# The root and reciprocal of a grouped RMS norm on four rows of 128 tokens, spread by way of DRAM, and a gate's Silu issued with the next eviction

## The chip, the cores and the metric

The kernel runs on one core of a Trainium2 chip. The metric is device time in microseconds (us), the median of repeated executions. Five engines run their own instruction streams: TensorE (PE in the profile, its weight loads PEld), VectorE (DVE), ScalarE (ACT), GpSimd (POOL) and SyncE (SP). In this kernel SP issues every DMA, in the order in which the program gives them to it.

## The reference

The input x is 2048 tokens by 1024 features. After a layernorm, two branches are added to it: a Mamba-2 block (64 heads of 64, 8 groups, state size 128, convolution over 4 tokens) and a base layer with a routed low-rank part. Cut to what matters here:

```python
proj = xn @ in_proj_w.T                     # gate 4096 | conv input 6144 | dt 64
xBC  = silu(causal_conv4(hbc) + conv_bias)
dt   = softplus(dt + dt_bias);  dA = exp(-exp(A_log) * dt)
state_t = state_{t-1} * dA_t + dt_t * x_t (outer) B_t
y_t  = state_t . C_t + D * x_t
# per group of 512 features and per token:
yn = y / sqrt(mean(y**2) + 1e-5) * norm_weight
yn = yn * silu(gate)
out = x + yn @ out_proj_w.T + (xn @ W_base.T + b_base + lora(xn))
```

The change touches the line of `yn = y / sqrt(...)` and the place where `silu(gate)` is computed.

## The kernel before

Features lie on partitions, tokens along the free axis. The sequence is cut into 2 parts s of 1024 tokens, each into 2 halves of 512 (TB) and 8 chunks of 128 (Q). A *block* is one (s, group, half): 32 blocks in order, each with four *slots* c = 0 to 3, one for each chunk of 128 tokens.

**The projection.** The in_proj matrix product runs as a stream of "products" of a seven-product scheme (Winograd's form of Strassen's). One product is four matmuls of 128x512 in f32, which the profile shows as 8 passes and some 3.4 to 3.6 us. The seven write three PSUM tiles (`ps_a`, `ps_x`, `ps_y`, with a suffix for what is computed: `x` conv input, `g` gate, `b` base; pool `ps_proj`, four buffers) in the order a1, x6, y5, a2, x7, y3, x4. A finished quarter of the result is *evicted* by `stored(...)`: for one quarter ACT applies the function straight to PSUM (L529); for the other three DVE adds a kept sum (L531) and, for the gate, ACT applies Silu in place (L533); then SP stores the tile (pool `ev`, four buffers) to DRAM. The last product of a tile triple, x4, needs the PSUM bank after the eviction behind x7.

**A slot.** Each slot holds four or five products. The loop over slots writes, in order: product 1 with its side work; in slot 0 the mean of the norm of the *previous* block (`norm_mean`); `scan_b`, the scan's matmuls of this chunk: 16 passes `ps_y`, 8 passes `ps_e`, and the state update `ps_st`; the loads of later decays (`load_decays`: `dab`, 512 KB spread to all partitions, and `ecp`, 2 x 128 KB); then the steps of `scan_a` for the next chunk (scan `es` on DVE L688; `ps_cb` and its copies on ACT L698, L700; `dab` on DVE L702; transposes `ps_xt`, the eight copies `xdt` scaled by dt on ACT L713, `xdd` on POOL L83) between products 2, 3 and 4. dt itself comes out of a softplus that DVE and ACT compute for a coming piece of the sequence (a polynomial from L318 on) spread over slots of the first half.

**Order.** PE's instructions keep the order of the program (`mm`, `transpose`). So do ACT's xdt copies and the conv's Silus, and in the second half of the sequence (s = 1) the POOL operations of `gp`. The remaining instructions of DVE, ACT and SP are put in order by a planner; the order is then fixed for each engine. The pool `ps_one` has one buffer for each of the tags "aux", "y", "e" and "st"; an instruction that writes into a tile of such a tag waits until all readers of the previous tile of that tag are done.

**The norm.** In the last slot of a block, `norm_squares` adds D x to y (into the tile xg of the conv) and sums the squares of the four 128-feature rows. In slot 0 of the next block `norm_mean` sums over partitions with one matmul against a 128x128 matrix of ones (f32, two passes, `ps_nv` in tag "aux"), which leaves the same 512 sums on all 128 partitions; ACT takes the root (L809). `norm_gate`, a generator advanced step by step with the side work of later products, takes the reciprocal (DVE L815), multiplies the four rows of xg (L818) and then multiplies by the gate (`sg`, L826), two rows at a time, each pair stored to DRAM as y. xg has two buffers (pool `p2`): the conv two blocks on first writes its buffer again with ACT (L640), DVE finishes it (L646). 

After about 2710 us of the profiled execution the second phase begins: out_proj, in a two-level form of the same scheme, with the low-rank part. The change doesn't touch it.

The functions that the change touches, and what calls them:

Of the kernel before, what the change touches and what calls it, by code (L numbers as in the profile page):

```python
# [8 lines left out]
F32 = mybir.dt.float32  # L9
AF = mybir.ActivationFunctionType  # L10
# [17 lines left out]
P = 128  # L28
TS = 1024
NS = L // TS  # L30
TB = 512
Q = 128
NQ = TB // Q
# [9 lines left out]
def mamba_lora_kernel(  # L43
# [17 lines left out]
    nc = tc.nc  # L61

    dram = ctx.enter_context(tc.tile_pool(name="dram", bufs=1, space=bass.MemoryType.DRAM))
    const = ctx.enter_context(tc.tile_pool(name="const", bufs=1))
# [6 lines left out]
    ps_one = ctx.enter_context(tc.tile_pool(name="ps_one", bufs=1, space=bass.MemoryType.PSUM))  # L71
    scan_ctx = ExitStack()
    p1 = scan_ctx.enter_context(tc.tile_pool(name="p1", bufs=1))
# [4 lines left out]
    def mm(*args, **kw):  # L78
        tc.keep_in_program_order(nc.tensor.matmul(*args, **kw))  # L79
# [11 lines left out]
    ones = const.tile([P, P], F32, name="ones")  # L91
    nc.vector.memset(ones, 1.0)
    ident = const.tile([P, P], F32, name="ident")
    make_identity(nc, ident)
    eps = const.tile([P, 1], F32, name="eps")
    nc.vector.memset(eps, EPS)


# [42 lines left out]
    nw = p1.tile([P, INNER // P], F32, name="nw")  # L141
# [151 lines left out]
    def small_mm(ps, x_of):  # L293
        for k in range(KT):
            mm(ps, x_of(k), wsm[:, k, :], start=(k == 0), stop=(k == KT - 1))
# [201 lines left out]
    def plain_pair(key, name, quarters, quarter):  # L497
# [22 lines left out]
            quarter(m, n, ps, rstd_of[n], ALU.mult)  # L520
        yield

    def stored(to, first_tile, s, func):


        def quarter(m, n, ps, add, alu=ALU.add):
            e = ev.tile([P, TB], F32, tag="ev", name="ev")
            if add is None:
                nc.scalar.activation(e, ps, func)  # L529
            else:  # L530
                nc.vector.tensor_tensor(e, ps, add, alu)  # L531
                if func != AF.Copy:
                    nc.scalar.activation(e, e, func)  # L533
            at = s * TS + n * TB
            nc.sync.dma_start(to[:, first_tile + m, at : at + TB], e)

        return quarter

# [66 lines left out]
    def steps(gen, n):  # L605

        return [lambda: next(gen, None) for _ in range(n)]


    xbc_of = {}  # L610
# [170 lines left out]
    def load_gate(s, g, half):  # L781
        sg = p1.tile([P, 4, TB], F32, tag="sg", name=f"sg_{s}_{g}_{half}")
        at = s * TS + half * TB
        nc.sync.dma_start(sg, gate_d[g][:, :, at : at + TB])
        sg_of[s, g, half] = sg

    norm_of = {}
# [14 lines left out]
        yield  # L802

    def norm_mean(s, g, half):
        y = y_of[s, g, half]
        ps = ps_one.tile([P, TB], F32, tag="aux", name=f"ps_nv_{s}_{g}_{half}")
        mm(ps, ones, y[:, 0, :], start=True, stop=True)
        std = p1.tile([P, TB], F32, tag="rms", name=f"rms_{s}_{g}_{half}")
        nc.scalar.activation(std, ps, AF.Sqrt, bias=eps, scale=1.0 / (4 * P))  # L809
        norm_of[s, g, half] = std  # L810

    def norm_gate(s, g, half):

        xg, std = xbc_of[s, g, half][0], norm_of[s, g, half]
        nc.vector.reciprocal(std, std)  # L815
        yield
        for j in range(4):
            nc.vector.scalar_tensor_tensor(  # L818
                xg[:, j, :], xg[:, j, :], nw[:, 4 * g + j : 4 * g + j + 1], std,
                ALU.mult, ALU.mult,  # L820
            )
        yield
        at = s * TS + half * TB
        for j in (0, 2):
            two = xg[:, j : j + 2, :]
            nc.vector.tensor_tensor(two, two, sg_of[s, g, half][:, j : j + 2, :], ALU.mult)  # L826
            nc.sync.dma_start(y_d[g][:, j : j + 2, at : at + TB], two)
            yield
# [137 lines left out]
    def target(slot):  # L966
        for (s0, p0), (s1, p1_) in zip(plan, plan[1:]):
            if slot <= s1:
                return p0 + (p1_ - p0) * (slot - s0) // (s1 - s0)
# [4 lines left out]
    for b, blk in enumerate(blocks):  # L974
        s, g, half = blk
        prev = blocks[b - 1] if b else None
        nxt = blocks[b + 1] if b + 1 < len(blocks) else None

        i, stage = divmod(b - 2, 3)
        piece, after = (1, i), stage  # L980
        if not (s == 0 and 0 <= i < NQ):
            piece = after = None
        if b == 14:
            ln_ctx.close()
            wo_ctx = ExitStack()
            wo = wo_ctx.enter_context(tc.tile_pool(name="wo", bufs=1, reuse_waits="tile"))
        if b == 15:
            base_left = left_sums
        if 0 <= b - 15 < 16:
            left_sums = out_sums(wo, b - 15)  # L990
        for c in range(NQ):
            slot += 1
            n = target(slot) - done
            follow = (*blk, c + 1) if c + 1 < NQ else (*nxt, 0) if nxt else None
            second = (*blk, c + 2) if c + 2 < NQ else (*nxt, c + 2 - NQ) if nxt else None
            side = []
            if c == 0 and nxt:
                side += [lambda: load_raw(*nxt)]
            if after == 0 and c == 1:
                load_piece(*piece, "sg", p1)  # L1000
                ln = ln_next(*piece)
            if after == 0 and c == 2:
                side += steps(ln, 3)
            if after == 0 and c == 3:
                side += steps(ln, 4)
            if after == 1 and c in (0, 2, 3):
                side += steps(rest, 1)
            if c in (1, 2) and nxt:
                if c == 1:
                    conv_steps = conv(*nxt)  # L1010
                side += steps(conv_steps, 4)
            if c == 2 and after != 0:
                side += [lambda: load_gate(*blk)]
            if b == 1 and c < 2:

                js = range(4) if c == 0 else range(4, 7)
                side[:0] = [
                    lambda j=j: nc.sync.dma_start(xop_d[0][j], ops_of["x", 0][j]) for j in js
                ]
            a = scan_a(*follow) if follow else iter(())  # L1020
            parts = [side[i * len(side) // n : (i + 1) * len(side) // n] for i in range(n)]

            products(1, parts[0])
            if c == 0 and prev:
                norm_mean(*prev)
            scan_b(*blk, c)
            if b == 14 and c:
                next(left_sums)
            if 0 <= b - 15 < 16 and c:
                next(left_sums)  # L1030
            if second:
                load_decays(*second)
            next(a, None)
            if c == 0 and prev:
                out = norm_gate(*prev)
                parts[1:4] = [[*p, lambda: next(out, None)] for p in parts[1:4]]
                parts[3] += [lambda: next(out, None)] * 2
            if c == NQ - 1:
                sq = norm_squares(*blk)
                parts[1] += steps(sq, 2)  # L1040
                parts[2] += steps(sq, 1)
            products(1, parts[1])
            next(a, None)
            products(1, parts[2])
            products(1, parts[3])
            next(a, None)
            if after == 0 and c == 1:
                next(ln)
            for i in range(4, n):
                products(1, parts[i])  # L1050
            if b == 14:
                left_sums = base_sums(wo, c)
                next(left_sums)
            if 0 <= b - 15 < 16 and c == 0:
                if b == 15:
                    next(base_left)
                next(left_sums)
            if after == 0 and c == 2:
                next(ln)
            if after == 0 and c == 3:  # L1060
                sm = lp.tile([P, 2, NSM], F32, tag="sm", name=f"sm_{piece[0]}_{piece[1]}")
                ps = ps_one.tile([P, 2, NSM], F32, tag="st", name=f"ps_sm_{piece[1]}")
                for h in range(2):
                    small_mm(ps[:, h, :], lambda k: piece_of[piece][:, k, h, :])
                nc.scalar.copy(sm, ps)
                rest = small(*piece, slice(piece[1], 2 * NQ, NQ), sm, home)
                load_gate(*blk)
            if (after, c) in ((1, 1), (2, 0)):
                next(rest)
    norm_mean(*blocks[-1])  # L1070
    for _ in norm_gate(*blocks[-1]):
        pass
# [157 lines left out]
    for t, (s, p) in enumerate(passes):  # L1230
        last = t + 1 == len(passes)
        for u, i in enumerate(units):
# [89 lines left out]
            for n, j in enumerate(inner):  # L1322
                w = w_ready.pop(0)
                ps = {1: pa, 2: pa, 6: px, 7: px, 4: px, 5: py, 3: py}[j]
                for q in range(2):
                    for k in range(KH):
                        mm(
                            ps[:, q, :], w[:, q, k, :], ops[j][:, k, :],
                            start=(n < 3 and q + k == 0), stop=(k == KH - 1), skip_group_check=True,
# [69 lines left out]
```

## Time and profile before

| | us |
|---|---|
| median of 3 runs | 3456.07 (3455.59 to 3456.18) |
| profiled execution | 3459.94 |
| its span, first to last instruction | 3458.2 |
| mean granted PE clock | 0.996 of full speed |
| PE busy | 3409.4, 12818 instructions |
| DVE busy | 2530.2 |
| ACT busy | 926.4 |
| POOL busy | 832.3 |
| DMA | 769.79 MB, mean 223 GB/s |

The profile is one execution with the time of each instruction. Rows of groups give the line, engine, operation, output and inputs by the program's names, shapes, count, busy time, mean duration in ns, and behind the last bar the idle time before them with what ended it. Rows of waits give who waited for whom: us in total, times, longest. The chain is followed back from the last instruction to whatever released each step. "issue" is time in which the engine waited for nothing that the profile shows. In a DMA row the last figure is the median time from issue to landing.

### The profile page before, as it was taken

What the parts mean: (1) busy time and instruction counts of PE and PEld (TensorE: products, weight loads), DVE (VectorE), ACT (ScalarE), POOL (GpSimd) and SP (SyncE); (2) the same over time, 40 slices, a digit from 0 to 9 for tenths busy, and PEclk for the clock granted to TensorE, in tenths of its full rate; (3) what the DMA queues carried; (4) which work ended last, traced back from release to release, by engine and by line L of the source; (5) the groups of instructions that cost most, each with busy time, mean ns of one, the idle gap of its engine ahead of it and who ended that gap; (6) DMA issues with size and microseconds to landing.
All of it is one profiled execution on the core that took longest, in us unless ns stands there. A gap on an engine that the chain in (4) does not pass through costs nothing.

```text
span 3458.2 us, 37638 instructions
## 1 busy us (share of the span) xinstructions
PE 3409.4 (99%) x12818; PEld 1993.4 (58%) x12818; DVE 2530.2 (73%) x2861; ACT 926.4 (27%) x2158; POOL 832.3 (24%) x571
## 2 busy tenths in 40 slices
PE   9999999999999999999999999999999999999999
PEld 7444544544545554444555555444445588888888
DVE  7548787877887877677888887777885466566665
ACT  2223343333433333323333333333331000000000
POOL 3133323233333211332332433322332000000000
PEclk9999999999999999999999999999999999999999
DMA  6546655655656676787787788787777687585644
GB/s 234 189 164 201 209 178 189 206 191 197 199 193 205 197 262 220 246 283 231 240 251 245 234 260 253 234 255 226 244 233 270 236 279 242 198 299 188 213 165 145
DMA packets 530319, 769.79 MB, mean 223 GB/s; under 512 B 35152, under 2 KB 264656, under 8 KB 527440
## 3 DMA queue, kind: packets, MB, share of 16 engines
q1 hardware_dynamic: 530128, 767.39, 68.6%
q8 instruction: 102, 1.67, 0.2%
q14 instruction: 89, 0.73, 0.1%
HBM read 516.64 MB, written 250.61 MB: 222 GB/s over the span
## 4 chain that ended last, share of the span: by engine, by line
PE 77%; DVE 10%; issue 6%; DMA 4%; POOL 2%; ACT 1%; SPq 0%; POOLq 0%; DVEq 0%; ACTq 0%
PE ps_x_x L79 10%; PE ps_x_w L79 8%; PE ps_a_x L79 7%; PE ps_y_x L79 7%; PE ps_x_g L79 6%; PE ps_a_w L79 6%; PE ps_y_w L79 6%; PE ps_y_g L79 4%; PE ps_a_g L79 4%; PE ps_y L79 3%; PE ps_e L79 3%; PE ps_x_b L79 2%; PE ps_st L79 2%; PE ps_a_b L79 2%; PE ps_y_b L79 2%
## 5 line engine op out<-in xcount | busy, mean ns | idle before, releaser
L688 DVE TENSOR_TENSOR_SCAN es<-dab,here 128x1024 f32<-128x1024 f32 x128 | 327.3, 2557 | 285.8 <-POOL xdd L83 264.6
L83 POOL TENSOR_TENSOR xdd<-xdt,es 128x512 f32<-128x512 f32 x128 | 145.3, 1135 | 1003.4 <-ACT xdt L713 967.6
L646 DVE SCALAR_TENSOR_TENSOR xg<-rawx,cw,xg 128x512 f32<-128x512 f32 x384 | 339.8, 934 | 22.3 <-ACT xg L640 21.7
L79 PE MATMUL ps_x_w<-t,w 128*128 128x256 f32 x1344 | 303.8, 379 | 0.0
L79 PEld LDWEIGHTS ps_x_w<-t,w 128*128 128x128 f32 x1344 | 255.4, 190 | 41.5 <-issue 7.7
L713 ACT ACTIVATE xdt<-ps_xt,dt 128x64 f32<-128x64 f32 x1024 | 223.2, 331 | 201.4 <-PE ps_xt L88 201.4
L83 POOL TENSOR_TENSOR wo<-wo 128x512 f32<-128x512 f32 (+1 forms) x112 | 214.1, 1912 | 16.6 <-DMA ecp<-run_d 10.3
L83 POOL TENSOR_TENSOR state<-state,tot 128x512 f32<-128x512 f32 x112 | 134.5, 1201 | 322.4 <-PE ps_e L79 311.0
L79 PE MATMUL ps_a_w<-q,w 128*128 128x256 f32 x896 | 202.5, 379 | 0.0
L702 DVE TENSOR_TENSOR dab<-es,cbm 128x1024 f32<-128x1024 f32 x128 | 174.1, 1360 | 27.5 <-ACT cbm L698 27.4
L1336 ACT COPY s<-ps_a_w 128x512 f32<-128x512 f32 x28 | 16.4, 585 | 636.2 <-PE ps_a_w L79 568.9
L79 PEld LDWEIGHTS ps_a_w<-q,w 128*128 128x128 f32 x896 | 170.2, 190 | 23.6 <-issue 0.5
L79 PEld LDWEIGHTS ps_y<-dab,xdt 128*64 128x64 f32 x2048 | 114.0, 138 | 109.6 <-issue 72.6
L79 PE MATMUL ps_y_x<-op_again,s_x 128*128 128x512 f32 x384 | 173.3, 594 | 0.0
L79 PE MATMUL ps_x_x<-op_again,s_x 128*128 128x512 f32 x384 | 172.7, 592 | 0.0
L79 PE MATMUL ps_a_x<-op_again,a_x 128*128 128x512 f32 x384 | 172.7, 592 | 0.0
L79 PE MATMUL ps_x_x<-op,s_x 128*128 128x512 f32 x368 | 165.5, 592 | 0.0
L79 PE MATMUL ps_y_x<-op,s_x 128*128 128x512 f32 x368 | 165.5, 592 | 0.0
L79 PE MATMUL ps_a_x<-op,a_x 128*128 128x512 f32 x368 | 165.4, 592 | 0.0
L646 DVE SCALAR_TENSOR_TENSOR bc<-rawb,cw,bc 128x512 f32<-128x512 f32 x192 | 159.1, 859 | 4.0 <-ACT bc L640 3.2
L79 PE MATMUL ps_y<-dab,xdt 128*64 128x128 f32 x2048 | 145.9, 283 | 13.4 <-ACT xdt L713 13.4
L79 PE MATMUL ps_e<-bc,state 128*128 128x128 f32 x960 | 142.1, 292 | 0.0
(236 smaller groups left out, 6050.7 us busy)
## 6 DMA issues: line engine op xcount, KB each, us to landing
w<-w SPq DMA_DIRECT2D x196, 512.0 KB, 3.7
dab<-da_d SPq DMA_DIRECT2D x128, 512.0 KB, 5.1
raw<-ev SPq DMA_DIRECT2D x192, 256.0 KB, 3.2
a_x<-in_w_in_dram SPq DMA_DIRECT2D x168, 256.0 KB, 4.2
w<-wo SPq DMA_DIRECT2D x96, 448.0 KB, 3.5
ecp<-run_d SPq DMA_DIRECT2D x256, 128.0 KB, 4.0
gate<-ev SPq DMA_DIRECT2D x128, 256.0 KB, 3.5
sg<-gate SPq DMA_DIRECT2D x32, 1024.0 KB, 7.3
```

The costliest lines, as they stand in the source:

```text
L79: tc.keep_in_program_order(nc.tensor.matmul(*args, **kw))
L83: ins = nc.gpsimd.tensor_tensor(*args)
L646: nc.vector.scalar_tensor_tensor(dst[:, i, :], raw[:, i, k : k + TB], cw[:, ti, k : k + 1], dst[:, i, :], ALU.mult, ALU.add,)
L688: nc.vector.tensor_tensor_scan(es.rearrange("p h t -> p (h t)"), dab.rearrange("p h t -> p (h t)"), here, 0.0, ALU.mult, ALU.add,)
L702: nc.vector.tensor_tensor(ms, es, cbm.unsqueeze(1).to_broadcast([P, HG, Q]), ALU.mult)
L713: ins = nc.scalar.activation(xdt[:, h, :], x_t[:, h, :], AF.Copy, scale=dt_of[s][:, half * NQ + c, at : at + 1],)
L1336: nc.scalar.copy(s1, pa)
```

## The change

1. `norm_mean` no longer multiplies with the matrix of ones. Four matmuls, one for each 128 tokens, use four columns of a narrow tile `row_of` that has ones in one column only, so that the sums of token range c land in row c of a [4, 128] PSUM tile. This tile takes tag "st" instead of "aux". ACT's root then runs on 4 partitions by 128 elements.
2. `norm_gate` takes the reciprocal on 4x128, writes the 2 KB to DRAM, and reads them back spread to all 128 partitions as [128, 512] (256 KB), both DMAs on SP. The multiplications with xg wait for this read.
3. The steps of `norm_gate` are advanced with products 2, 4 and the last of the slot (one, one and two steps), where it was products 2, 3 and 4 (one, one and three steps).
4. In `stored`, where DVE adds and ACT then applies a function (the gate's Silu), the ACT instruction and the store are no longer issued at once but put on a list, which the next eviction empties first.

The epsilon tile becomes a column of `row_of`. Over the whole program SP issues 64 more DMAs, and PE 192 more passes.

```diff
+    row_of = const.tile([P, 8], F32, name="row_of")
+    nc.vector.memset(row_of, 0.0)
+    nc.vector.memset(row_of[:, NQ - 1 : NQ], 1.0)
+    eps = row_of[:, 7:8]
...
+    waiting = []
     def stored(to, first_tile, s, func):
         def quarter(m, n, ps, add, alu=ALU.add):
+            for fn in waiting:
+                fn()
+            waiting.clear()
             e = ev.tile([P, TB], F32, tag="ev", name="ev")
...
                 nc.vector.tensor_tensor(e, ps, add, alu)
-                if func != AF.Copy:
+            def rest():
+                if add is not None and func != AF.Copy:
                     nc.scalar.activation(e, e, func)
-            nc.sync.dma_start(to[:, first_tile + m, at : at + TB], e)
+                nc.sync.dma_start(dst, e)
+            if add is not None and func != AF.Copy:
+                waiting.append(rest)
+            else:
+                rest()
...
-        ps = ps_one.tile([P, TB], F32, tag="aux", name=f"ps_nv_{s}_{g}_{half}")
-        mm(ps, ones, y[:, 0, :], start=True, stop=True)
-        std = p1.tile([P, TB], F32, tag="rms", name=f"rms_{s}_{g}_{half}")
-        nc.scalar.activation(std, ps, AF.Sqrt, bias=eps, scale=1.0 / (4 * P))
-        norm_of[s, g, half] = std
+        ps = ps_one.tile([NQ, Q], F32, tag="st", name=f"ps_nv_{n}")
+        for c in range(NQ):
+            mm(
+                ps, row_of[:, NQ - 1 - c : 2 * NQ - 1 - c], y[:, 0, c * Q : (c + 1) * Q],
+                start=(c == 0), stop=(c == NQ - 1),
+            )
+        rms = p1.tile([P, TB], F32, tag="rms", name=f"rms_{n}")
+        std = rms[0:NQ, 0:Q]
+        nc.scalar.activation(std, ps, AF.Sqrt, bias=eps[0:NQ], scale=1.0 / (4 * P))
+        norm_of[s, g, half] = rms
...
         nc.vector.reciprocal(std, std)
+        std_d = dram.tile([NQ, Q], F32, tag=f"std_d_{n}", name=f"std_d_{n}")
+        nc.sync.dma_start(std_d, std)
+        nc.sync.dma_start(
+            rms, std_d.rearrange("c t -> (c t)").unsqueeze(0).to_broadcast([P, TB])
+        )
         yield
         for j in range(4):
             nc.vector.scalar_tensor_tensor(
-                xg[:, j, :], xg[:, j, :], nw[:, 4 * g + j : 4 * g + j + 1], std,
+                xg[:, j, :], xg[:, j, :], nw[:, 4 * g + j : 4 * g + j + 1], rms,
...
-                parts[1:4] = [[*p, lambda: next(out, None)] for p in parts[1:4]]
-                parts[3] += [lambda: next(out, None)] * 2
+                for i, k in ((1, 1), (3, 1), (n - 1, 2)):
+                    parts[i] += [lambda: next(out, None)] * k
```

## The prediction, made before the changed kernel ran

> **What bounds the kernel now.** I read three things in this order: busy shares and the chain's shares, then the waits of TensorE (PE), then the rows of what the change touches. First the page (engine, busy us, share of the span, instructions; below it the chain that ended last by engine):
>
> ```profile
> PE 3409.4 (99%) x12818; PEld 1993.4 (58%) x12818; DVE 2530.2 (73%) x2861; ACT 926.4 (27%) x2158; POOL 832.3 (24%) x571
> ...
> PE 77%; DVE 10%; issue 6%; DMA 4%; POOL 2%; ACT 1%; SPq 0%; POOLq 0%; DVEq 0%; ACTq 0%
> ```
>
> PE idles only 3458.2 - 3409.4 = about 49 us. No other engine can set the time by its sum; another engine's instruction counts only where it ends a PE wait, or creates one. The waits of PE (who waited for what: us in total, times, longest), and below them three of other engines:
>
> ```profile
> PE ps_y L79 <- ACT xdt L713: 13.4, 5, 6.8
> PE ps_nv L79 <- ACT xdt L713: 10.0, 4, 2.7
> PE ps_st L79 <- POOL xdd L83: 5.4, 1, 5.4
> ...
> PE ps_x_g L79 <- DVE ev L531: 2.7, 4, 1.3
> ...
> PE ps_x_x L79 <- DVE ev L531: 1.7, 4, 0.6
> ...
> ACT ev L533 <- DVE ev L531: 152.5, 50, 8.0
> ...
> ACT rms L809 <- PE ps_nv L79: 47.4, 16, 9.2
> ...
> ACT xg L640 <- DMA y<-xg: 58.3, 20, 8.8
> ```
>
> So the change can gain at most the first two rows and the two ev rows, 13.4 + 10.0 + 2.7 + 1.7 = 28 us, 0.8% of the time. Losses have no such ceiling. The rows of the norm (busy us, mean ns of one | idle before), and the DMA rows nearest to the new round trip (KB, median us from issue to landing):
>
> ```profile
> L815 DVE RECIPROCAL rms<-rms 128x512 f32<-128x512 f32 x32 | 107.0, 3344 | 6.5 <-ACT rms L809 6.5
> ...
> L318 DVE RECIPROCAL u<-u 128x128 f32<-128x128 f32 x4 | 3.8, 954 | 0.0
> ```
> ```profile
> dab<-da_d SPq DMA_DIRECT2D x128, 512.0 KB, 5.1
> ...
> s_x_d<-s_x SPq DMA_DIRECT2D x96, 256.0 KB, 2.1
> s_x<-s_x_d SPq DMA_DIRECT2D x96, 256.0 KB, 4.9
> ```
>
> **Part 1, the reciprocal: less DVE work, worth little as such.** 3344 ns becomes about 954 (same free size, fewer partitions): 32 x 2.39 = 76 us off DVE. PE doesn't wait for DVE's sum, so this counts only through what follows sooner. It does in the first half: PE's ps_y waits at 451.69, 703.81, 955.68 and 1206.02 (6.76 + 1.33 + 2.74 + 2.11 = 12.94 us) end with xdt, whose scale dt comes from a polynomial on DVE queued behind the norm. With DVE 2.4 us ahead there, three go and some 2 us stay of the longest if two further DVE steps move with it: **-10.9** (bounds -7, the three short ones and a little, to -12.9).
>
> **Part 2, the gate's Silu goes to the next eviction.** Four ps_nv waits in the second half (1584.63, 2177.61, 2328.00, 2480.90: 2.73 + 2.10 + 2.44 + 2.69 = 9.96) come from ACT: a Silu stands in front of the eight xdt copies and itself waits for DVE's addition (the row "ACT ev L533 <- DVE ev L531"). Issued one eviction later it lies behind them. ps_nv then starts at once, but its root becomes the next thing due (part 3) and is a little late in three of these blocks (0.6, 0.2, 0.4): **-8.8** (bounds -10 to -6). The Silu is needed by the gate's reload slots later; its ev buffer is held some 4 to 7 us longer in a cycle of four buffers in about 28 us, so the delay is covered. One 1.3 us wait (ps_x_g at 801.76) is taken up by part 3's delay of PE ahead of it: **-1.3**.
>
> **Part 3, the bank.** ps_nv moves from "aux" to "st", a pool with one buffer per tag. ps_st, the state update of the same slot, uses "st" too and follows ps_nv on PE by only about 2.9 us (ps_y and ps_e lie between). It must now wait until ACT's root has read ps_nv. Behind ps_st in PE's order stand all products, so each us of it is a us of the end. One such block in the timeline (start, duration, instruction, idle before it):
>
> ```profile
> 767.20 1.02 PE L79 MATMUL ps_st<-xdd,bt 128*128 128x512 f32 x2
> 767.35 0.63 ACT L533 ACTIVATE ev<-ev 128x512 f32<-128x512 f32 x1 [4.50 <-DVE ev L531]
> ...
> 768.00 1.28 ACT L809 ACT_TABLE_LOAD   x1
> ...
> 769.29 0.69 ACT L809 ACTIVATE rms<-ps_nv,eps 128x512 f32<-128x512 f32 x1
> ```
>
> The root ends at 769.98, 2.78 us after ps_st's start. Done the same way for all 32 blocks, the root ends too late in seven (their reciprocals start at 433.6, 690.4, 770.0, 941.8, 1191.9, 1273.0, 1741.7): 3.48 + 2.11 + 2.78 + 2.06 + 2.11 + 2.39 + 4.05 = 18.98; elsewhere 0.1 to 2.2 us remain. What stands in front of the root on ACT in these seven is the same in the changed order: a Silu already waiting for an eviction in three, a conv that waits for its load in one, a chain of small DVE steps in three. The root itself shrinks from 687 ns to about 290 (near the 261 ns of a 128x128 copy, L698), -0.4 each, and a semaphore hop adds 0.06: **+16.6** (bounds +8 to +19). In return ps_cb no longer waits for the root, which cost 0.5 us of weight loads and no PE time.
>
> **Part 4, the matmul.** Two passes of 512 columns (0.95 us from the first ps_nv to ps_y) become 8 passes of 128. Rows of ps_xt and ps_e show 0.11 to 0.125 us for one such pass: 0.88 to 1.0. **0** (bounds -2 to +2 over 32).
>
> **Part 5, the round trip by DRAM.** Before, the first scaling (L818) starts 3.4 to 6.1 us after the reciprocal, since DVE has other work between. Now it must wait for: reciprocal 0.95, SP's issue 0.3, the write 2.1, and the spread read. The read moves 256 KB into SBUF; the nearest row is s_x<-s_x_d, the same bytes reread just after a write, 4.9 (by halves dab, ecp: 4.1 in the first, 5.0 in the second). First scaling at 0.95 + 0.3 + 2.1 + 4.1 = 7.5, in the second half 8.4. Ahead of the write in SP's order stand the decay loads, of which ecp waits for the y of L760; behind the read's wait on the write stand weight and decay loads (2 us later, normally landed many us ahead). The last product with the gate (L826) ends 13.2 to 13.5 after the reciprocal instead of 11 to 12, so some 1.6 to 2.5 later, as is the y store. What is late next is the chain here (start, duration, what):
>
> ```profile
> 1026.25 3.66 DVE xg L818 x4
> ...
> 1030.44 2.36 DVE xg L826 x2
> ...
> 1032.81 4.94 DMA y<-xg
> ...
> 1037.86 0.82 ACT xg L640
> ...
> 1051.17 0.67 DVE ev L531
> ...
> 1051.88 3.70 PE ps_x_x L79 x8
> ```
>
> xg has two buffers: the next conv's first multiply on ACT (L640) waits for the store of y (20 of 30 blocks in the waits), the conv on DVE follows, then the eviction that frees a PSUM tile for PE. At 1051.88 PE already waited 0.48, so there is no slack and the whole 1.7 us is lost. Setting the shift against the slack of each block's eviction gives losses in eight: 517: 1.2; 1021: 1.7; 1273: 1.0; 1590: 2.3; 1960: 3.5 (the eviction misses a place behind a scan); 2104: 1.7; 2333: 0.7; 2485: 1.8; sum **+13.9**, and 0.6 where an eviction stands right behind the scaling: **+14.5**. For each us more of the trip about 8 to 14 are added, for each us less 8 saved. Bounds 0 (the trip as short as the slack) to +32.
>
> The Trainium skill's page "DMA: Bandwidth & Descriptors" (section "Anatomy of one DMA — SWDGE (gpsimd) path") puts the fixed cost of a DMA at about 2.0 us and the rest at bytes by bandwidth; 2 KB out and 256 KB in would be an estimated 2.0 + 2.6 = 4.6, so the first scaling starts at 5.9, within what DVE's order leaves anyway. By the rule part 5 is 0 and the sum ends near 3452; by the rows (2.1 and 4.9 under this kernel's own load of 223 GB/s) it is +14.5. The rule was fitted on DMAs issued by GpSimd, and its page shows no load beside them; I take the rows. The same page's "Two DMAs through the same engine are not ordered" says why the read can't be issued behind the write without waiting; the added order of SP shows that wait, and its price is the 2.1 row.
>
> **Sum** against the profiled 3459.94 (span 3458.2, 1.7 around it): -10.9 - 8.8 - 1.3 + 16.6 + 0 + 14.5 = +10.1. The profiled execution is 3.9 above the median; the difference carried to it: 3456.07 + 10 = **3466**.
>
> **Rivals.**
> (a) *The trip is hidden.* DVE's order, made anew, puts evictions and scan work in the gap, and the shift stays under the slack. For it: the rule above, and 22 blocks where I find slack. Against: the zero slack at 1051.88 and its like. Parts 1 to 4 alone: -21.0 + 16.6 = -4.4, so 3452: no change that could be told.
> (b) *The root is in time, and it gets faster.* If moving Silus lets the root in the three Silu blocks start within 2.2 us of ps_nv (from there it decides: 2.9 less its 0.3 and hops), part 3 is 8.1 instead of 16.6 and part 5, with these blocks not displaced, about 4: -21.0 + 8.1 + 4 = -9, so 3447. For: the Silu is what the change moves. Against: a Silu moved from one eviction lands on the next, and 50 of them wait for DVE now.
> (c) *Late landings on SP's queue.* The read lands 1.5 us later (5.6 after a write of 3.2, both inside the spread of the rows, where ecp loads go up to 8.8). Part 5 grows by 1.5 x 14 = 21: 3487.
>
> **How the numbers follow.** A difference under 0.2% (6.9 us) can't be told from none. Main case 0.45, its own range 3460 to 3474, of which the part under 3463 (0.12) is within 0.2%; (a) 0.20, within; (b) 0.20, faster; (c) 0.15, slower. So faster 0.20, same 0.12 + 0.20 = 0.32, slower 0.33 + 0.15 = 0.48. The range 3444 to 3486 reaches over (b) to its low end and takes most of the way to (c), leaving out about 2 in 10.
>
> **What would show it.** Parts 1 and 2: the rows of ps_y and ps_nv waiting for xdt fall below 4 us together. Part 3: a new row of ps_st waiting for the root, six to ten times, up to 4 us; if it isn't there, (b). Part 5: L818 idle before its first instruction for a DMA in nearly all of 32; "PE ps_x <- DVE ev" in the second half from 4.4 to above 15 us; if L818 waits but that row stays, (a). The prediction is wrong if DVE's order around the scaling differs from the old one so far that other evictions fall behind the waiting L818, which stalls everything after it on DVE.

## The result and the profile after

The changed kernel takes 3480.14 us (median of 6 runs, 3477.35 to 3485.84), the kernel before 3456.15 beside it (6 runs, 3455.59 to 3458.61): ratio 1.0070, 95% interval 1.0057 to 1.0083, 24 us slower. The profiled execution is the shortest of the six, 3477.35 (span 3475.5), 17.4 above the profiled one before; readings below are of that pair unless they say "median".

The page of the changed kernel (same columns as before):

```profile
PE 3416.2 (98%) x13010; PEld 1999.0 (58%) x13010; DVE 2460.2 (71%) x2863; ACT 915.9 (26%) x2157; POOL 836.0 (24%) x571
```

DVE is 70 us less busy, ACT 10, and the span is 17 us longer. PE has 10 us more of idle time (span less busy time: 59.3 in place of 48.8) and 7 us more of busy time, though the 192 more passes are short ones: ps_nv costs 33.2 us in the row below, 33.3 before. The waits of PE, and three of other engines:

```profile
PE ps_st L79 <- ACT rms L833: 21.7, 10, 3.5
PE ps_x_x L79 <- DVE ev L542: 8.7, 5, 2.3
PE ps_st L79 <- POOL xdd L83: 5.2, 1, 5.2
PE ps_x_g L79 <- DVE ev L542: 5.0, 5, 1.7
...
PE ps_mean L79 <- DVE half L187: 3.9, 2, 3.2
...
PE ps_y L79 <- ACT xdt L730: 1.0, 1, 1.0
```
```profile
ACT ev L546 <- DVE ev L542: 122.5, 39, 6.6
...
ACT xg L657 <- DMA y<-xg: 74.1, 21, 8.4
...
DVE xg L849 <- DMA rms<-std_d: 54.9, 23, 6.7
```

The first row is new: the state update waits for the root of the norm, in 10 blocks of 31. The rows of xdt fell from 23.4 us to 1.0. The waits of ps_x for an eviction rose from 4.4 to 13.7. The rows of the norm, with the read behind them (KB, median us to landing):

```profile
L849 DVE SCALAR_TENSOR_TENSOR xg<-xg,nw,rms 128x512 f32<-128x512 f32 x128 | 92.9, 773 | 55.0 <-DMA rms<-std_d 54.9
...
L79 PE MATMUL ps_nv<-y,row_of 128*4 128x128 f32 x256 | 33.2, 273 | 0.0
...
L841 DVE RECIPROCAL rms<-rms 4x128 f32<-4x128 f32 x32 | 29.9, 934 | 16.3 <-ACT rms L833 16.3
...
L833 ACT ACTIVATE rms<-ps_nv,row_of 4x128 f32<-4x128 f32 x32 | 11.4, 358 | 49.7 <-PE ps_nv L79 49.5
```
```profile
rms<-std_d SPq DMA_DIRECT2D x32, 256.0 KB, 3.8
```

One of the ten blocks, in the second half, first ACT, then PE (start, duration, instruction, idle before it):

```profile
1588.20 0.63 ACT L546 ACTIVATE ev<-ev 128x512 f32<-128x512 f32 x1 [2.68 <-issue]
1590.98 0.63 ACT L546 ACTIVATE ev<-ev 128x512 f32<-128x512 f32 x1 [2.15 <-DVE ev L542]
1591.63 1.28 ACT L833 ACT_TABLE_LOAD   x1
1592.92 0.36 ACT L833 ACTIVATE rms<-ps_nv,row_of 4x128 f32<-4x128 f32 x1
```
```profile
1587.04 1.04 PE L79 MATMUL ps_nv<-y,row_of 128*4 128x128 f32 x8
...
1593.42 1.27 PE L79 MATMUL ps_st<-xdd,bt 128*128 128x512 f32 x2 [3.24 <-ACT rms L833]
1594.49 5.16 PE L79 MATMUL ps_x_g<-op_again,a_g 128*128 128x512 f32 x8
1599.49 0.38 PE L79 MATMUL ps_cb<-bc 128*128 128x128 f32 x2
```

Before the change this block had ps_nv waiting 2.73 us for xdt (at 1584.63), with both Silus done by 1585.1. Now ps_nv starts at once; both Silus stand between it and its root, the second one waiting for an eviction that DVE does behind a scan, and ps_st waits 3.24 us. The product behind it (1594.49) takes 5.16 us where the same eight passes take 3.60 elsewhere. That is not in any row of waits. It counts as busy time, and the windows over the 3.5 us behind five such stalls show what it is (start:end, length, busy time of the five engines with counts, then the granted clock of TensorE, DMA share and GB/s):

```profile
436.35:439.85 3.50, 3.50 (x5) 1.45 (x6) 3.50 (x8) 1.36 (x2) 0.00 (x0) 0.61 0.03 10
1593.42:1596.92 3.50, 3.50 (x5) 1.47 (x6) 2.06 (x3) 0.00 (x0) 0.00 (x0) 0.61 0.59 175
1748.36:1751.86 3.50, 3.50 (x5) 1.62 (x6) 2.06 (x3) 0.00 (x0) 0.00 (x0) 0.59 0.55 152
2345.16:2348.66 3.50, 3.50 (x5) 1.50 (x6) 2.06 (x3) 0.00 (x0) 0.00 (x0) 0.51 0.53 162
2498.84:2502.34 3.50, 3.50 (x5) 1.54 (x6) 2.06 (x3) 0.00 (x0) 0.00 (x0) 0.53 0.65 182
```

The granted clock is 0.51 to 0.61 there. Against the same instructions before, ps_cb behind these five stalls comes another 1.5 to 1.8 us late, on top of the stall: about 8 us in all.

Not all of these 8 us is a loss against the kernel before, which has such stretches too. There the clock fell below 0.8 behind five stalls, here behind seven (these five, and those at 641.89 and 1477.86). Four of the old ones are gone (behind 451.69, 1206.02, 1584.63 and 2328.00), and by the same comparison of equal instructions that gives back an estimated 4 to 6 us, while the new one at 641.89 adds some 1.4. So the slow clock explains about 4 to 5 of the 7 us of busy time; another 1 us comes at the very start, where the first group of ps_mean takes 10.10 us in place of 9.10.

### The profile page after: what moved, and what is told of

Same layout as the page of the kernel before. It is cut to its first block, busy times and chain, and to the rows that moved or that the text cites. A ratio compares the mean times of both kernels' runs of the same rounds, so it can differ in the third digit from the quotient of the medians.

```text
span 3475.5 us, 38185 instructions
## 1 busy us (share of the span) xinstructions
PE 3416.2 (98%) x13010; PEld 1999.0 (58%) x13010; DVE 2460.2 (71%) x2863; ACT 915.9 (26%) x2157; POOL 836.0 (24%) x571
## 4 chain that ended last, share of the span: by engine, by line
PE 58%; DVE 3%; issue 3%; DMA 2%; POOL 1%; ACT 1%; SPq 0%; POOLq 0%; DVEq 0%; ACTq 0%
PE ps_x_w L79 8%; PE ps_x_x L79 6%; PE ps_y_w L79 6%; PE ps_a_w L79 6%; PE ps_y_x L79 4%; PE ps_a_x L79 4%; PE ps_x_g L79 4%; PE ps_a_g L79 3%; PE ps_y_g L79 3%; PE ps_x_b L79 2%; PE ps_e L79 2%; PE ps_y L79 2%; PE ps_st L79 2%; PE ps_a_b L79 2%; PE ps_y_b L79 2%
## 5 line engine op out<-in xcount | busy, mean ns | idle before, releaser
L1367 ACT COPY s<-ps_a_w 128x512 f32<-128x512 f32 x28 | 16.4, 585 | 633.5 <-PE ps_a_w L79 566.1
L79 PE MATMUL ps_st<-xdd,bt 128*128 128x512 f32 x240 | 128.5, 618 | 26.9 <-ACT rms L833 21.7
```

Source lines behind the costliest of these rows:

```text
L1367: nc.scalar.copy(s1, pa)
```

## The experiments

My theory after seeing this: the bank costs most (21.7 us of root waits and 8 of slow clock), the trip by DRAM the rest (late evictions), and the deferred Silu is a gain that the bank turns around. The rivals: the trip is the main loss; or the deferral is harmful in itself. Runs of one group shared a chip and its runs of the kernel before; across groups compare ratios.

| kernel | median us | before beside it | ratio, 95% interval |
|---|---|---|---|
| changed | 3480.14 | 3456.15 | 1.0070, 1.0057 to 1.0083 |
| e1: sums in "aux" | 3456.05 | 3455.66 | 1.0000, 0.9991 to 1.0008 |
| e2: Silu not deferred | 3473.12 | 3455.66 | 1.0052, 1.0037 to 1.0067 |
| e3: deferred Silu alone | 3441.47 | 3455.66 | 0.9960, 0.9945 to 0.9974 |
| e4: old step hooks | 3476.91 | 3455.66 | 1.0059, 1.0044 to 1.0074 |
| e5: e3 with wide sums in "st" | 3485.00 | 3458.77 | 1.0073, 1.0058 to 1.0088 |
| e6: scaling doesn't wait for the trip | 3497.27 | 3458.77 | 1.0113, 1.0096 to 1.0130 |
| e7: ps_st one product later | 3465.12 | 3458.77 | 1.0020, 1.0013 to 1.0027 |
| e8: filler ahead of ps_st | 3490.58 | 3458.77 | 1.0091, 1.0075 to 1.0106 |
| e9: filler behind the sums | 3470.11 | 3456.79 | 1.0038, 1.0026 to 1.0051 |
| e10: e3 with the trip, wide | 3502.72 | 3456.79 | 1.0134, 1.0120 to 1.0148 |
| e11: e1 without the deferral | 3465.26 | 3456.79 | 1.0026, 1.0017 to 1.0035 |
| e12: e3 with new step hooks | 3439.10 | 3459.67 | 0.9945, 0.9932 to 0.9959 |

### e1: the bank undone

```diff
-        ps = ps_one.tile([NQ, Q], F32, tag="st", name=f"ps_nv_{n}")
+        ps = ps_one.tile([NQ, Q], F32, tag="aux", name=f"ps_nv_{n}")
```

> The changed kernel with one word different: the four-row sums go to the PSUM bank 'aux' again, as before the change, in place of 'st'. Theory (most of the loss is the state update ps_st waiting for the root, and the slower TensorE clock behind each such wait over 3 us): the 21.7 us of waits go, and with them some 8 us of slow products behind the five longest, so about 3452, with no row 'ps_st <- ACT rms' and no stretch of granted clock near 0.6 behind a norm. Rival (the way by DRAM and the late evictions behind it cost as much or more): the waits of ps_x for an eviction stay or grow, and it doesn't fall below 3470.

Measured: 3456.05, level with the kernel before, 24 us below the changed one. Its waits of PE:

```profile
PE ps_x_x L79 <- DVE ev L542: 8.8, 6, 3.0
PE ps_x_g L79 <- DVE ev L542: 7.2, 6, 3.1
PE ps_st L79 <- POOL xdd L83: 4.5, 1, 4.5
PE ps_mean L79 <- DMA piece<-in_xT_dram: 4.3, 1, 4.3
PE ps_y L79 <- ACT xdt L730: 4.1, 1, 4.1
PE ps_mean L79 <- DVE half L187: 4.1, 3, 3.0
```

The root row is gone, and what took its place is small: 3 us more at ps_y, 2 more at ps_x. The bank is worth 24 us, a whole change's loss, where the trip is the same. That is shown by one word of difference, with one reserve: the order of some DVE and SP instructions moved with it.

### e2: the Silu not deferred, and e11: the same in "aux"

e2 is the changed kernel with `stored` as it was before; e11 is e2 with tag "aux".

> The changed kernel without its last part: the gate's Silu is issued at once, as before. Theory (the late Silu is what now stands in front of the root in the blocks of the second half: three waits of about 3.2 us with 1.6 us of slow clock each, 14 us): these go, and in their place ps_y waits for the xdt behind a Silu in four places, about 1.8 us each, 7 us; so 3473. Rival (the deferral is a gain wherever it is): 3487 or more.

> The four-row norm with the way by DRAM and the moved steps, sums in 'aux' as before the change, Silu issued at once as before. Theory (the parts add up: four rows and the trip cost 14.6 us, as between the two kernels with the deferred Silu): 3456 + 14.6 = 3471. Rival (the four-row norm is harmless where Silu isn't deferred): 3456 within 4.

e2: 3473.12, the number expected, but its terms only in part. In the blocks at 1593, 2346 and 2497 the root wait is 0.76 us each where the changed kernel has 3.08 to 3.24, and the row of root waits falls from 21.7 to 15.3. Against that, ps_y waits 2.3 us for xdt, less than the 7 expected, and two shorter stalls (1273.85, 2151.69) now have a slow clock behind them. e11: 3465.26, between the two expectations: without deferral the four-row norm with its trip costs 0.26% or 9 us in "aux", not 14.6. So the parts don't simply add up; they do in a table of four (ratios of e11, e1, e2 and the changed kernel):

| | Silu at once | Silu deferred | deferral |
|---|---|---|---|
| four rows, "aux" | 1.0026 | 1.0000 | -9 us |
| four rows, "st" | 1.0052 | 1.0070 | +6 us |
| bank | +9 us | +24 us | |

In "aux" a deferral takes the four waits of ps_nv for xdt away (10.0 us in e11's waits, none in e1's). In "st" ps_nv doesn't wait for xdt anyway (e2, which doesn't defer, has no such row): the bank alone ends these waits. What the Silu then delays is the root, and in "st" PE waits for that. The +6 by itself is not clear of noise, since the intervals of e2 and the changed kernel overlap; that it differs from the -9 is.

### e3: the deferred Silu alone, and e12: with the moved hooks

e3 is the kernel before with the list in `stored`. e12 adds the new places of the steps of `norm_gate`, with root, reciprocal and scaling as before.

```diff
-                parts[1:4] = [[*p, lambda: next(out, None)] for p in parts[1:4]]
-                parts[3] += [lambda: next(out, None)] * 2
+                for i, k in ((1, 1), (3, 1), (n - 1, 2)):
+                    parts[i] += [lambda: next(out, None)] * k
```

> The kernel before with the deferred Silu alone. Theory (it takes the Silu out from in front of xdt, and with the sums in 'aux' a late root holds up no matmul): the four waits of ps_nv for xdt, 10.0 us, go and nothing takes their place, 3446. Rival (the deferral moves evictions and roots on VectorE and ScalarE so that other waits come): 3456 or more.

> The kernel before with the deferred Silu and the norm's second half hung on products 2, 4 and the last, as in the changed kernel; root, reciprocal and scaling as before, without the way by DRAM. Theory (the hooks matter little, since the planner orders VectorE by what is ready; they moved the changed kernel by 3 us): 3441.5 within 4. Rival (later scaling lets the dt steps and evictions go first, and the waits of ps_y for xdt, 11.9 us, shrink): 3434 or less.

e3: 3441.47, 14 us faster than before, 4.5 more than expected. No row of ps_nv is left; the rest of PE's waits is nearly as before. Two of the four old waits (1584.63 and 2328.00, of 2.73 and 2.44 us) had a slow clock behind them (0.61, 0.72), which goes as well. e12 is level with e3 or some us better (the intervals overlap): 3439.10, ratio 0.9945, the fastest kernel of this study. Its waits at ps_y (11.9 us in e3):

```profile
PE ps_y L79 <- ACT xdt L726: 7.2, 3, 6.3
```

The deferral is no harm in itself: that rival falls. Taken one after another, the parts are -14 us for the deferral (e3), +14 for the four-row norm with its trip and the new hooks (e1), and +24 for the bank.

### e4: the old hooks in the changed kernel

> The changed kernel with the steps of the norm's second half hung on products 2, 3 and 4 as before, not on 2, 4 and the last. Theory (the planner orders VectorE by what is ready, and the read's landing sets the scaling): 3480 within 7. Rival (the later hooks are what keeps evictions ahead of the waiting scaling): VectorE waits for the read for clearly more than 55 us and evictions come late, 3495 or more.

3476.91, within the 7 us; the root waits are 21.8 us, DVE waits 54.5 us for the read (54.9 in the changed kernel). The places of the steps decide little.

### e5: the bank with the wide sums

```diff
-        ps = ps_one.tile([P, TB], F32, tag="aux", name=f"ps_nv_{s}_{g}_{half}")
+        ps = ps_one.tile([P, TB], F32, tag="st", name=f"ps_nv_{s}_{g}_{half}")
```

> The kernel before with the deferred Silu, and its wide sums (128x512, no way by DRAM) in bank 'st' in place of 'aux'. Theory (the bank alone makes ps_st wait for the root; four rows or 128 make little difference): root waits of 21.7 us plus 0.33 us each for the longer root, and 8 us of slow clock behind the five longest, on the 3441.5 of the kernel with the deferred Silu alone: about 3470, with a row 'ps_st <- ACT rms' of 20 us or more. Rival (the waits come with the four-row form, by its different order on ScalarE): 3445.

3485.00: the bank alone, without four rows or trip, costs 1.0073 - 0.9960 = 1.13% or 39 us, more than the 29 expected.

```profile
PE ps_st L79 <- ACT rms L822: 26.7, 10, 3.7
```

26.7 us are root waits in the same blocks. Behind five of these, of 2.37 to 3.68 us, the clock falls to between 0.52 and 0.69, with ps_cb another 1.5 to 1.8 us late each time. The four-row form isn't what makes the root late; ps_st's place 2.9 us behind the sums is. What the bank costs depends on what else stands in front of the root: 9 us (e11 to e2), 24 (e1 to the changed kernel) or 39 (here).

### e6: the scaling without the trip

```diff
+    flat = ones[:, 0:1].to_broadcast([P, TB])
-                xg[:, j, :], xg[:, j, :], nw[:, 4 * g + j : 4 * g + j + 1], rms,
+                xg[:, j, :], xg[:, j, :], nw[:, 4 * g + j : 4 * g + j + 1], flat,
```

> The changed kernel, but the scaling multiplies by ones and so doesn't wait for the root spread by DRAM (the division by the root is left out; the root, the reciprocal, the write and the spread read are all still done). Theory (the trip makes evictions late, as the prediction's part 5 has it, +14.5): ps_x waits for an eviction fall from 13.7 us to about 4, 3466. Rival (the trip is hidden behind other work of VectorE): within 4 us of the 3480 of the changed kernel.

3497.27, slower than both expectations. The evictions behaved as the theory has it: ps_x waits fell from 13.7 to 8.0 us. But the scaling, free of its wait, changed the order of DVE over the whole kernel, and 12 roots are late for 38.1 us in place of 10 for 21.7. It tells nothing of the trip's cost; taking a dependency away let the planner lay out another kernel.

### e10: the trip without the shorter reciprocal

```diff
         nc.vector.reciprocal(std, std)
+        std_d = dram.tile([1, TB], F32, tag=f"std_d_{s}_{g}_{half}", name=f"std_d_{s}_{g}_{half}")
+        nc.sync.dma_start(std_d, std[0:1, :])
+        nc.sync.dma_start(std, std_d.to_broadcast([P, TB]))
```

> The kernel before with the deferred Silu, the wide root and reciprocal in 'aux' as before, and behind the reciprocal the way by DRAM: one row of 512 is written (2 KB) and read back spread over 128 partitions, and the scaling waits for it. It has the trip without the shorter reciprocal. Theory (the trip delays y, the conv behind it and the evictions): scaling at 3.35 + 6.5 = about 9.9 us after the reciprocal's start, 2.4 later than on four rows; ps_x waits for an eviction rise from 6 us to 30 or more and nothing is gained at ps_y, so 3441.5 + 30 = 3472 or more. Rival (VectorE's other work hides the trip, and what the four-row form loses comes from its order): within 5 us of 3441.5.

3502.72: 1.0134 - 0.9960 = 1.74%, 60 us over e3, twice the 30 expected. The first scaling starts at a median of 10.5 us after the reciprocal in the first half and 10.2 in the second (e3: 5.2 and 6.1; expected 9.9), and the waits of PE are:

```profile
PE ps_x_g L79 <- DVE ev L538: 14.5, 5, 4.4
PE ps_x_x L79 <- DVE ev L538: 12.3, 7, 4.9
PE ps_mean L79 <- DVE half L183: 10.2, 2, 5.6
PE ps_st L79 <- POOL xdd L83: 8.1, 4, 5.3
PE ps_y L79 <- ACT xdt L726: 6.6, 1, 6.6
PE ps_mean L79 <- DVE rawx L632: 6.2, 2, 3.2
```

Evictions went from 6.0 to 26.8, and there are losses I hadn't expected: the layernorm of the coming pieces, which DVE does between, comes late for PE (ps_mean, 16.4 us), and ten stalls have a slow clock behind them where e3 has three. The trip does reach PE, so the rival that hides it falls. Against e1 (scaling at 7.8 and 8.2) e10 is 1.34% or 46 us slower; 2.5 of that are at ps_y. Over 2.0 to 2.7 us of later scaling this is some 18 us for each us, slow clock and ps_mean with it, where the prediction took 8 to 14. But e10's reciprocal also keeps DVE 2.4 us longer each time, so this slope is not the trip's alone.

### e7: ps_st a product later

In slot 0 the state update (matmul, POOL's and DVE's parts) was issued after product 2.

> The changed kernel, but in slot 0 the state update ps_st with what follows it is issued one product later; the sums stay in bank 'st'. Theory (only the nearness of ps_st to the sums makes the wait): a product of 3.4 us covers roots that were up to 3.5 us late, no row 'ps_st <- ACT rms' over 1 us, no slow clock behind it: 3480 - 21.7 - 8 = 3450. Rival (the later state makes the next chunk's work late by as much): 3470 or more.

3465.12 (ratio 1.0020): 17 us below the changed kernel by ratio, half of the 30 expected. The root row is 0.3 us, and no slow clock follows a norm. But ps_x waits for evictions 20.0 us in place of 13.7, and ps_mean for DVE 8.1 in place of 3.9: PE, without its stalls, runs into the late evictions of the trip, and the later state moved DVE's work too. The two are not told apart here.

### e8 and e9: more work against the slow clock

```diff
+        if (s * G + g) * 2 + half in (2, 16, 18, 26, 28):
+            for i in range(9):
+                mm(whole[:, 1, :], ones, ones, start=True, stop=True, skip_group_check=True)
```

e9 has these lines between the sums and the root (`whole` is the bank's tile, of which the sums use another part); e8 had them between ps_e and ps_st.

> The changed kernel with more work: in the five blocks in which ps_st waits over 3 us for the root, nine needless matmuls of 128x128 (18 passes, about 2 us) stand ahead of ps_st and write to an unused part of the same bank. Theory (TensorE idle for over 3 us lowers its granted clock for the next product, 1.5 to 1.8 us each): the waits shrink to about 1.2 us, the clock stays at 1.0 behind them, and the kernel is faster by 5 x 1.6 = 8 us, 3472. Rival (the slow products have another cause, such as late operands): 3480 or more.

> The changed kernel with more work: in the five blocks in which ps_st waits over 3 us for the root, nine needless matmuls (18 passes of 128, about 2 us) are issued right behind the sums and ahead of the root, into an unused part of the same bank. The root stands behind a Silu on ScalarE until later than they end, so it isn't delayed; ps_y, ps_e and ps_st come 2 us later, and ps_st waits some 1.2 us for the root instead of 3.2. Theory (TensorE idle for about 3 us lowers its granted clock for the next product, 1.5 to 1.8 us each): the clock stays at 1.0 behind these waits, and the kernel is faster than the changed one by 5 x 1.6 = 8 us, 3472. Rival (the slow products have another cause): 3480 or more.

e8 did not test it: its fillers write into the tile that the root reads and so waited for the root themselves (15.8 us at five places), and PE stalled as long as before, with the fillers on top. In e9 they go ahead. It does 5 x 2.2 = 11 us of needless work and is *faster* than the changed kernel: 1.0038 (1.0026 to 1.0051) against 1.0070 (1.0057 to 1.0083), 11 us. The five filled stalls are 0.87 to 1.70 us, and the windows behind them:

```profile
435.04:438.54 3.50, 3.50 (x8) 1.60 (x9) 3.50 (x9) 0.00 (x0) 0.00 (x0) 1.00 0.11 44
1594.89:1598.39 3.50, 3.50 (x8) 1.60 (x9) 2.56 (x4) 0.00 (x0) 0.09 (x1) 1.00 0.49 145
1747.65:1751.15 3.50, 3.50 (x8) 1.59 (x9) 2.56 (x4) 0.00 (x0) 0.08 (x1) 1.00 0.49 140
2343.52:2347.02 3.50, 3.50 (x8) 1.60 (x9) 2.56 (x4) 0.00 (x0) 0.26 (x1) 1.00 0.51 144
2495.74:2499.24 3.50, 3.50 (x8) 1.59 (x9) 2.56 (x4) 0.00 (x0) 0.13 (x1) 1.00 0.46 142
773.47:776.97 3.50, 3.50 (x5) 1.44 (x6) 2.06 (x3) 0.00 (x0) 0.00 (x0) 0.52 0.55 166
```

Eight passes in 3.5 us where there were five. Behind each of the five, ps_cb comes 1.4 to 1.7 us sooner relative to ps_st: 8.15 us together. That the idle time causes the slow clock is shown for these five: with it filled, the clock stays. The last line is a stall that was not filled: 2.33 us, clock 0.52; in the changed kernel the same stall, of 2.32 us at 775.97, left the clock at 1.00. This one and another unfilled stall (1274.01, 1.95 us, clock 0.69) cost e9 1.7 us each that the changed kernel didn't pay, so in the profiled pair the gain is 5.0 us; only the medians lie 11 apart.

## Why the prediction was right or wrong

The forecast was 3466, slower, in the range 3444 to 3486; it is 3480. The direction held, and so did the mechanisms of parts 1, 3 and 5; that of part 2 did not. The size was 10 us by forecast, 17.4 by the profiled pair, 24 by the medians. By its own steps:

- *Part 1, -10.9.* The mechanism is right: ps_y's waits for xdt fell by 12.4 us, and of the four only 1.03 us at 454.7 is left. Some 3 us of this is not the reciprocal's: the root wait at 436.35 delays PE just ahead, and in e1, without it, 4.1 us are left at this place. The reciprocal takes 934 ns (954 taken).
- *Part 2, -8.8.* This is the step that failed: "Issued one eviction later it lies behind them. ps_nv then starts at once, but its root becomes the next thing due (part 3) and is a little late in three of these blocks (0.6, 0.2, 0.4)". ps_nv does start at once. But with xdt done early the scan no longer waits for POOL's xdd (2.92 us at 1591.83 in e2, which doesn't defer) and stands ahead of the second eviction in DVE's order, in e1 and e3 too. So in those three blocks the Silu comes late, and makes ps_st wait 3.24, 3.08 and 3.19 us for the root instead of 1.2 together. Of the 10.0 us gained, 9.5 came straight back; three new slow stretches cost 5 more, and two old ones gave back about 3. Counted between equal instructions ahead of and behind the four blocks, they lose 1.5 us where the forecast gained 8.8. Nor did these waits need the deferral: part 3's move to "st" ends them by itself (e2). e1, e2, e3 and e11 show this: the deferral is worth -14 us alone, -9 with the four-row norm in "aux", and nothing or a loss (+6, within noise) in "st".
- *Part 3, +16.6.* The mechanism is right and is the main loss. In the seven blocks named the waits are 3.52, 0.50, 2.32, 0, 0.50, 1.93 and 3.25: 12.0 us. Three of them, where I put the root behind a chain of small DVE steps, came nearly in time. That DVE had more room there is likely but not shown; in e5, with the wide reciprocal, two of the three wait 2.19 and 0.94 us. The root takes 358 ns, not 290.
- *Slow clock, not in the sum.* No term of the forecast had it: 8 us behind the five long root waits, an estimated 4 net of the stretches that came and went elsewhere. The sign of it was there before: the windows behind the waits at 451.69 and 1473.05 had a clock near 0.5.
- *Part 4, 0.* Right: 0.96 us from ps_nv to ps_y where it was 0.95 without the wait.
- *Part 5, +14.5, with -1.3.* The trip was sized well: first scaling at a median of 7.7 us in the first half and 8.5 in the second (7.5 and 8.4 forecast), the last product with the gate at 13.6 and 13.9 (13.2 to 13.5). What it costs was put too high: evictions make PE wait 9.3 us more than before. They are late at six of the eight blocks named (517, 1021, 1590, 1960, 2104, 2485), where the waits grew by 8.4 us and not the 12.2 forecast; not at 1273 and 2333; and at 297 and 614 besides (1.2 us each). ps_mean adds 2.2. The sign asked for, ps_x above 15 us in the second half, did not come: it is 7.4 there. Its starting value, 4.4, was that of the whole run; the second half alone had 2.1. The scaling waited for the read in 23 blocks, not in nearly all of 32. The choice between rows and rule was the right one: by the rule that the prediction takes from the Trainium skill's page "DMA: Bandwidth & Descriptors" (an estimated 4.6 us for both DMAs) the first scaling would start at an estimated 5.9 us here and 8.2 in e10. It started at 7.7 to 8.5 and at 10.2 to 10.5. Within the trip, the read lands faster than I took it (3.8, not 4.1 to 5.0) but is issued later: a median of 4.1 us after the reciprocal's start, where 0.95 + 0.3 + 2.1 gives 3.35.
- *Rivals.* (a), the hidden trip, is refuted by the waits for evictions here and by e10. (b) was half right: some roots were in time, others, by the moved Silu itself, late. (c) didn't happen: all 32 reads landed within 3.6 to 4.0 us.

PE's idle time grew by 10.5 us, which is near the forecast sum by chance: part 2 gained less, parts 3 and 5 lost less in the places named. The other 7 us of the profiled pair are busy time, over half of it at a low clock. The medians lie 24 apart because the profiled run of the changed kernel is the shortest of its six, and that of before, 3459.94, lies above all of its own.

## What to carry to other kernels

When a result moves to another buffer, list who writes that buffer next and how soon: here the next writer came 2.9 us behind, the reader stood last in another engine's queue, and that cost 24 us where the forecast's gains together were 21. A deferred instruction is free only if what then follows it isn't needed soon; test each part alone and with the others, since the same deferral gained 14 us alone, 9 beside the four-row norm in one bank, and nothing in the other. An engine's saved busy time (70 us of DVE here) is worth nothing but the waits that it ends.

## What the runs showed that I had not expected

A stall of PE can cost more than its length. Over the thirteen profiles of the two kernels and of e1 to e11 (stalls of 0.9 us or more, after the first 200 us), the granted clock in the 3.5 us behind the stall fell below 0.8 in

| length of the stall, us | stalls | with a slow clock |
|---|---|---|
| 0.9 to 1.93 | 83 | 0 |
| 1.93 to 3.0 | 48 | 25 |
| 3.0 to 4.0 | 39 | 34 |
| over 4.0 | 27 | 27 |

Behind five root waits of the changed kernel and five of e5 this cost 1.5 to 1.8 us each beyond the stall. The Trainium skill, page "TensorE: Matmul & The Clock Gate", section "Part 1: The HAM clock gate (the "warmup" mystery)", has a monitor with free-running windows of about 3.4 us and advises against idle gaps above that. The free-running part fits what is seen, that equal stalls of 2.32 us have it in one run and not in another; as a limit 3.4 us is too high here, since half of the stalls of 2 to 3 us are hit. This may also make a kernel with many stalls near 2 to 3 us spread more: the six runs of the changed kernel cover 8.5 us, those of before 3.0. The mean granted clock of the changed kernel's six is 0.996 in the shortest and 0.993 in the longest, which fits; that the stalls make the difference is argued, not shown.
